# Expert values of an attention + mixture-of-experts kernel: from resident tiles to a DRAM scratch that is read back pair by pair

## The chip, the cores and the metric

The kernel runs on one core of a Trainium2 chip. The metric is the device time of one launch in microseconds (us). The kernel before took 1017.82 us, the median of three runs (1015.98 to 1018.09).

Names of the engines: PE is TensorE (matmuls; PEld its weight loads), DVE is VectorE, ACT is ScalarE, POOL is GpSimd, SP is SyncE, which in this kernel issues every DMA, in one queue and in program order.

## The reference

Eight sequences of 1024 tokens with 256 features pass one layer: attention in a linear form, a layer norm, a gated feed-forward block with 16 experts, a second layer norm.

```python
# attention: x is (8, 1024, 256)
qkv = x @ Wqkv + bqkv;  q, k, v = split(qkv)
q = q - q.mean(2);  k = k - k.mean(2)
q2 = q*q / (sum(q*q) + 1e-7);  q2 = q2 / norm(q2, over the features)
k2 = k*k / (sum(k*k) + 1e-7);  k2 = k2 / norm(k2, over the tokens)
kv = einsum('bnc,bnd->bcd', k2, v)
att = (v + einsum('bnc,bcd->bnd', q2, kv) / sqrt(N)) @ Wln + bln
x = layernorm(x + att)
# experts: E = 16, H = 128, D = 256
sel    = sigmoid(einsum('bsd,ed->bse', x, expert_sel))
scores = relu(einsum('bsd,edh->bseh', x, keys))
out    = einsum('bseh,ehv,bse->bsv', scores, values, sel)
x = layernorm(x + out)
```

All is float32. The last layer norm takes off the mean over the features, so the kernel takes the mean off the rows of `values` beforehand; "centered values" are these rows.

## The kernel before, in words

**Tiles and chunks.** The 8192 tokens are cut into 16 chunks of 512 (`CH`). Features lie on the partitions, tokens in the free dimension. Every float32 operand of a large product is split into a high and a low part (`h` and `l`), and a product is three matmuls: high by high, low by high, high by low.

**The expert part of a chunk.** For expert e, ffn1 (six matmuls of 512 columns, line 358) makes the hidden tile `h` from `keyh`, `keyl` and the normed tokens `ych`, `ycl`. `gated` (lines 1052 to 1057) then does three steps: DVE multiplies relu(h) by the gate, which lies broadcast over the partitions in `selb`; ACT copies the high part `sh`; DVE makes the low part `sl`. ffn2 (six matmuls, line 1137) multiplies `sh` and `sl` by the centered values `valh` and `vall` and adds into two PSUM tiles, `w0` and `w1`, over all 16 experts of the chunk. Experts go in pairs p = 0 to 7. From chunk 1 on, pairs 4 to 7 make their hidden tiles by a scheme with fewer products (`fast1`, lines 1075 to 1111, matmuls on line 1090), which needs sums of keys (`u_sums`, from a second load `ksr` of the keys) and of tokens (`u_t`).

**Everything else of a chunk** is spread among the expert pairs of an earlier chunk: the projections `kp` and `qp`, the products `ap` (tokens by squared keys) and `yp` (attention output), the transposes `qt`, the gates `sp`, and the column sums of the layer norms `yv` and `wv`.

**Who sets the order.** The functions only declare tasks (`add`) with an engine, a cost, a key (when it is wanted) and the buffers that they read and write. `Work.order` (lines 202 to 319) lays them out once, before anything is issued, and what it decides is the program order on every engine: an engine whose next instruction waits holds up all that is behind it. A buffer is given a tag, and each tag has a number of slots (`SB_SLOTS`, lines 41 to 44); a task that opens a buffer is placed only when a slot is free, and the real instruction waits on the last user of that slot.

**Values before the change.** `u_weights(g, key)` (lines 941 to 976) runs four times in chunk 0, for experts 4g to 4g+3. It loads keys (`kst`) and values (`vst`) through staging slots, splits the keys into `keyh` and `keyl`, takes the mean of each row of the values (`vst_m`), and writes `valh` (ACT, line 972) and `vall` (DVE, line 974). The tags `g0` to `g3` have four slots each of 4 KB per partition: two for keys and two for values. They stay for the whole kernel, so that ffn2 of all 16 chunks reads the same eight value tiles. `g2` and `g3` serve as staging for chunk 0 first (`kst`, `vst` of group 0; the tokens `xf`, `nf` of chunks 0 and 1).

**Other buffers that matter here.** `ld2` has three slots of 2 KB and holds, one after the other, `kst`, `vst`, `xf`, `nf` and `ksr`. `selb` has two slots: the gate rows of a pair are fetched from DRAM (`gates_of`, line 1030) when DVE has done the gates of the pair two before.

Of the kernel before, what the change touches and what calls it, by code (L numbers as in the profile page):

```python
# [23 lines left out]
LAG = 2.2  # L24
# [6 lines left out]
FAST_FROM = 1  # L31
FAST_AT = 0.39
AT_Y, AT_YEND, AT_X, AT_N, AT_K, AT_Q, AT_M, AT_END = 2.04, 4.17, 0.95, 0.19, 5.21, 12, 16.28, -0.91
AT_Q1, AT_K2, AT_W1, AT_W2, AT_W3, AT_SUMS, AT_SEL = -30, -19.9, -10.93, -7.7, 8.8, 8.58, 7
EAGER = 3.73
BOOST = 2.0
RESERVE = {"att": 1}
# [2 lines left out]

SB_SLOTS = {
    "ld2": 3, "xh": 2, "xl": 2, "s4": 4, "ych": 2, "ycl": 2, "sh": 2, "sl": 2, "selb": 2, "gt": 2, "t4": 6, "t2": 4,
    "v1": 2, "g0": 4, "g1": 4, "g2": 4, "g3": 4, "acc": 1, "asb": 1, "mh": 1, "ml": 1, "tiny": 14,
}
PS_SLOTS = {"h": 4, "att": 2, "w0": 1, "w1": 1}

# [1 line left out]
def f(ap):  # L48
    return ap.bitcast(F32)
# [273 lines left out]
def attn_ffn_kernel(ctx, tc, x, xT, wqT, wk, wvT, wlnT, bcols, brows, selT, keys, values, outT):  # L323
# [13 lines left out]
    def sbuf(tag, shape, name, dtype=F32):  # L337
        return work.buf(tag, shape, dtype, name)
# [75 lines left out]
        cbuf("bc", [P, 8]), cbuf("bkbc", [P, 1, D]), cbuf("bqbc", [P, 1, D]), cbuf("by", [P, 2]), cbuf("bvlbc", [P, D]),  # L414
    )
    eft, ewt, bls, blt = cbuf("eft", [P, 2, NE]), cbuf("ewt", [P, 2, P], FR), cbuf("bls", [P, 1]), cbuf("blt", [P, 1])
    keyh, keyl, valh, vall = {}, {}, {}, {}

    S.preload_act_table_set("natural_log_exp_and_others")

# [96 lines left out]
    def split(c, key, name, src, h, l, width):  # L517

        rows = h.shape[1]
        n = 1 if c < 2 else 2  # L520
        for i in range(n):
            s = slice(i * rows // n, (i + 1) * rows // n)
            part = None if n == 1 else i
            b = sbuf("g3" if c < 2 else "ld2", [P, rows // n, width], f"{name}{c}_{i}")
            add("D", 2.1 / n, key, lambda b=b, s=s: nc.sync.dma_start(out=b.ap, in_=src(s)), w=[b])
# [413 lines left out]


    def u_weights(g, key):
        for to, name in ((keyh, "keyh"), (keyl, "keyl"), (valh, "valh"), (vall, "vall")):
            to[g] = sbuf(f"g{g}", [P, 4, 2, P] if to in (keyh, keyl) else [P, 4, D], f"{name}{g}", FR)
        n = 1 if g == 0 else 2
        size = 4 // n
        for i in range(n):
            here = slice(i * size, (i + 1) * size)
            es = slice(4 * g + here.start, 4 * g + here.stop)
            tag = "g2" if g == 0 else "ld2"
            part = here if n > 1 else None  # L950
            kst = sbuf(tag, [P, size, 2, P], f"kst{g}_{i}")
            add("D", 2.1 / n, key, lambda kst=kst, es=es: nc.sync.dma_start(out=kst.ap, in_=keys[es].rearrange("e (k p) h -> p e k h", p=P)), w=[kst])
            add("S", c_act(size * D, plain=True), key + 1.2, lambda kst=kst, here=here: S.copy(keyh[g][:, here], kst.ap), r=[kst], w=[(keyh[g], part)])
            for j in range(2 // n):
                two = slice(here.start + 2 * j, here.start + 2 * j + 2)
                apply(key + 1.5, lambda two=two: keyl[g][:, two], lambda kst=kst, j=j: kst[:, 2 * j : 2 * j + 2], lambda two=two: f(keyh[g][:, two]),
                      ALU.subtract, CH, [kst, (keyh[g], part)], [(keyl[g], two)], "V" if g == 0 else spare(key))
        key += 1
        for i in range(n):
            here = slice(i * size, (i + 1) * size)  # L960
            es = slice(4 * g + here.start, 4 * g + here.stop)
            tag = "g2" if g == 0 else "ld2"
            vst = sbuf(tag, [P, size, D], f"vst{g}_{i}")
            add("D", 2.1 / n, key, lambda vst=vst, es=es: nc.sync.dma_start(out=vst.ap, in_=values[es].rearrange("e h v -> h e v")), w=[vst])
            m = tiny(f"vst{g}_{i}_m")
            for j in range(2 // n):
                two = slice(2 * j, 2 * j + 2)
                add("V", c_dve(CH), key + 1.2, lambda two=two, vst=vst, m=m: V.tensor_reduce(m[:, two], vst[:, two], AX.X, ALU.add), r=[vst], w=[(m, j)])
            add("V", 0.17, key + 1.3, lambda m=m: V.tensor_scalar(m[:, :size], m[:, :size], -1.0 / D, None, ALU.mult), r=[m], w=[m])
            for j in range(size):  # L970
                e = here.start + j
                add("S", c_act(D), key + 1.4, lambda j=j, e=e, vst=vst, m=m: S.activation(valh[g][:, e], vst[:, j], AF.Identity, bias=m[:, j : j + 1]),
                    r=[vst, m], w=[(valh[g], e)])
                add("V", c_dve(D, ptr=True), key + 1.8, lambda j=j, e=e, vst=vst, m=m: V.scalar_tensor_tensor(
                    vall[g][:, e], vst[:, j], m[:, j : j + 1], f(valh[g][:, e]), ALU.add, ALU.subtract),
                    r=[vst, m, (valh[g], e)], w=[(vall[g], e)], port=True)

# [55 lines left out]
    def u_pair(c, p):  # L1033
        key = NE * c + 2 * p
        if p == 0:
            wps[c] = [psum(f"w{v}_{c}", f"w{v}") for v in range(2)]
        gates_of(c, p, max(0, SOON - 2 * p) if c == 0 else 0)
        sel = selb[c, p]
        a, b = (sbuf(n, [P, 2, CH], f"{n}{c}_{p}", FR) for n in ("sh", "sl"))
        if c >= FAST_FROM and p in FAST_PAIRS:  # L1040
            fast1(c, p, key, sel, a, b)
        else:
            for i in range(2):
                plain1(c, 2 * p + i, key + i, sel, a, b)
# [67 lines left out]

    def ffn2_halves(c, e, key, a, b):

        g, i = e // 4, e % 2
        if e == NE - HALVED:
            rest[:] = [psum(f"rest{v}") for v in range(2)]

        def run(part):
            r = slice(part * CH // 2, (part + 1) * CH // 2)  # L1120
            for j, (w, x) in enumerate(((valh[g], a), (vall[g], a), (valh[g], b))):
                for v in range(2):
                    out = rest[v][:, : CH // 2] if part else wps[c][v][:, r]
                    T.matmul(out, w[:, e % 4, v * P : (v + 1) * P], x[:, i, r], start=part == 1 and e == NE - HALVED and j == 0,
                             stop=e == NE - 1 and j == 2)

        for part in range(2):
            add("T", c_mm(CH // 2, 6), key + LAG + part * HALVED, lambda part=part: run(part),
                r=[(valh[g], e % 4), (vall[g], e % 4), (a, i), (b, i)], w=rest if part else wps[c])

    def ffn2(c, e, key, a, b):
        g, i = e // 4, e % 2

        def run():
            for j, (w, r) in enumerate(((valh[g], a), (vall[g], a), (valh[g], b))):
                for v in range(2):
                    T.matmul(wps[c][v].ap, w[:, e % 4, v * P : (v + 1) * P], r[:, i], start=e == 0 and j == 0, stop=e == NE - 1 and j == 2)  # L1137

        t = add("T", c_mm(CH, 6), key + LAG, run, r=[(valh[g], e % 4), (vall[g], e % 4), (a, i), (b, i)], w=wps[c])
        if c == 0 and e < SOON:  # L1140
            work.goals[t] = -2.8 * e

# [263 lines left out]
```

## Time and profile before

| what | value |
|---|---|
| time, median of three runs | 1017.82 us (1015.98 to 1018.09) |
| profiled execution, span from first to last instruction | 1013.8 us |
| what lies around the span (median less span) | 4.0 us |
| PE busy | 1003.8 us |
| DVE, ACT, POOL busy | 792.9, 678.5, 488.5 us |
| DMA queue of SP | 98.48 MB, 30.4% of the 16 DMA engines' time |
| DMA issues of SP | 372 |
| granted TensorE clock, mean | 0.996 |

The page gives each engine's busy time, the DMA queues, the chain that ended last (followed back from the last instruction to what released each step) and the costliest groups of instructions. A matmul's end is modelled, so that a busy PE is not yet a PE at its pace; the distance from one matmul's start to the next shows the pace. The views used below are the table of stretches (busy time of each engine between two times, granted clock, share of the DMA engines), the timeline of one engine, the list of waits and the chain in order of time. All times in them count from the start of the span.

### The profile page before, as it was taken

Reading aid. Unit: us, or ns where it says so; the run is one execution under the profiler, and the core shown is the slowest. Engines: PE = TensorE matmul, PEld = TensorE weight load, DVE = VectorE, ACT = ScalarE, POOL = GpSimd, SP = SyncE. Lnnn points to the kernel's source line nnn. Section 1 sums busy time; section 2 is a strip of 40 time slices with the busy share of each in tenths; the row PEclk is TensorE's granted clock in tenths of the full one; section 3 lists DMA queues with packets and bytes.
Section 4 is the critical chain, followed back from the end, with each engine's and each line's share of the span. In section 5 each row is a group of like instructions: output and inputs, shape, how many; then the busy total and the mean of one; then the engine's idle time right before and its main releaser. Section 6 shows DMA issues by size and latency. Waiting matters only on the chain.

```text
span 1013.8 us, 16268 instructions
## 1 busy us (share of the span) xinstructions
PE 1003.8 (99%) x5709; PEld 868.9 (86%) x5709; DVE 792.9 (78%) x1363; ACT 678.5 (67%) x1515; POOL 488.5 (48%) x436
## 2 busy tenths in 40 slices
PE   9999999999999999999999999999999999999996
PEld 9978879888898988889888888988889888888886
DVE  7889888588776887768887688867888688686775
ACT  7767576676776767767676676757776675665543
POOL 1001685538564474655636475454754537333430
PEclk9999999999999999999999999999999999999998
DMA  6144433322241333323223232323323222223131
GB/s 203 56 124 125 120 98 118 94 97 93 83 126 65 116 94 104 99 89 97 94 91 110 86 105 70 116 96 102 105 75 104 94 85 75 93 85 105 64 125 42
DMA packets 65298, 99.52 MB, mean 98 GB/s; under 512 B 6336, under 2 KB 24896, under 8 KB 65216
## 3 DMA queue, kind: packets, MB, share of 16 engines
q1 hardware_dynamic: 65216, 98.48, 30.4%
q8 instruction: 45, 0.74, 0.3%
q14 instruction: 37, 0.30, 0.1%
HBM read 89.54 MB, written 8.91 MB: 97 GB/s over the span
## 4 chain that ended last, share of the span: by engine, by line
PE 92%; DVE 3%; POOL 2%; DMA 1%; ACT 1%; issue 1%; SPq 0%; POOLq 0%; DVEq 0%; ACTq 0%
PE w L1137 32%; PE h L358 17%; PE hx L1090 11%; PE yp L358 8%; PE qp L358 4%; PE hy L1090 4%; PE kp L358 4%; PE ap L358 4%; PE qt L771 1%; PE sp L358 1%; PE pm L358 1%; DMA ksr<-keys 1%; PE warm L435 0%; DVE sl L1057 0%; DMA xf<-xT 0%
## 5 line engine op out<-in xcount | busy, mean ns | idle before, releaser
L1137 PE MATMUL w<-sh,valh 128*128 128x512 f32 x504 | 157.9, 394 | 0.0
L1137 PE MATMUL w<-sh,vall 128*128 128x512 f32 x504 | 157.8, 394 | 0.0
L1137 PE MATMUL w<-sl,valh 128*128 128x512 f32 x504 | 157.6, 394 | 0.0
L1055 DVE SCALAR_TENSOR_TENSOR h<-h,selb 128x512 f32<-128x512 f32 x136 | 93.9, 692 | 29.6 <-PE h L358 24.9
L1137 PEld LDWEIGHTS w<-sl,valh 128*128 128x128 f32 x504 | 94.6, 188 | 22.4
L1137 PEld LDWEIGHTS w<-sh,vall 128*128 128x128 f32 x504 | 94.6, 188 | 22.0
L1056 ACT CAST sh<-h 128x512 fp32r<-128x512 f32 x136 | 74.2, 588 | 57.2 <-PE w L1137 46.2
L358 PE MATMUL h<-ych,keyh 128*128 128x512 f32 x272 | 110.4, 406 | 0.0
L358 PE MATMUL h<-ycl,keyh 128*128 128x512 f32 x272 | 108.3, 398 | 0.0
L358 PE MATMUL h<-ych,keyl 128*128 128x512 f32 x272 | 107.5, 395 | 0.0
L1057 DVE TENSOR_TENSOR sl<-h,sh 128x512 fp32r<-128x512 f32 x136 | 87.7, 682 | 22.4 <-ACT sh L1056 22.3
L1137 PEld LDWEIGHTS w<-sh,valh 128*128 128x128 f32 x504 | 86.0, 188 | 10.9
L389 POOL TENSOR_TENSOR k<-k,ks 128x512 f32<-128x512 f32 x25 | 30.9, 1256 | 102.4 <-DVE ks L566 102.4
L1109 DVE TENSOR_TENSOR hx<-hx,p 128x512 f32<-128x512 f32 x60 | 41.8, 696 | 29.9 <-ACT hy L1106 29.6
L389 POOL TENSOR_TENSOR ysq<-ysq 128x512 f32<-128x512 f32 x15 | 20.0, 1333 | 89.2 <-ACT ysq L891 89.2
L1151 POOL TENSOR_TENSOR w<-w,ycl 128x512 f32<-128x512 f32 x30 | 38.3, 1297 | 49.4 <-DVE w L1148 49.4
L358 PEld LDWEIGHTS h<-ych,keyl 128*128 128x128 f32 x272 | 51.5, 189 | 12.2
L358 PEld LDWEIGHTS h<-ycl,keyh 128*128 128x128 f32 x272 | 51.6, 190 | 10.7
L358 PEld LDWEIGHTS h<-ych,keyh 128*128 128x128 f32 x272 | 51.5, 189 | 10.9
L893 DVE SCALAR_TENSOR_TENSOR ycl<-yp,by,ych 128x512 fp32r<-128x512 f32 x32 | 24.0, 750 | 41.4 <-ACT ysq L891 41.4
L389 POOL TENSOR_TENSOR kss<-kss 128x512 f32<-128x512 f32 (+1 forms) x18 | 25.0, 1391 | 57.6 <-DVE gr L935 57.6
L1057 DVE TENSOR_TENSOR sl<-hx,sh 128x512 fp32r<-128x512 f32 x60 | 40.8, 681 | 15.1 <-ACT sh L1056 14.9
(511 smaller groups left out, 3204.6 us busy)
## 6 DMA issues: line engine op xcount, KB each, us to landing
selb<-sel SPq DMA_DIRECT2D x253, 256.0 KB, 3.4
xf<-xT SPq DMA_DIRECT2D x30, 256.0 KB, 2.8
outT<-w SPq DMA_DIRECT2D x15, 512.0 KB, 3.0
nf<-x SPq DMA_DIRECT2D x28, 256.0 KB, 4.7
kst<-keys SPq DMA_DIRECT2D x6, 256.0 KB, 3.3
vst<-values SPq DMA_DIRECT2D x6, 256.0 KB, 3.0
nf<-x SPq DMA_DIRECT2D x2, 512.0 KB, 7.6
ksr<-keys SPq DMA_DIRECT2D x4, 256.0 KB, 3.6
```

The costliest lines, as they stand in the source:

```text
L358: T.matmul(out, w, r, start=first and i == 0, stop=last and i == len(terms) - 1)
L389: fns = {e: (lambda e=e: ENG[e].tensor_tensor(out(), a(), b(), op)) for e in engines}
L771: T.transpose(o[:, t * P : (t + 1) * P], q[:, t, ct * P : (ct + 1) * P], ident.ap)
L893: add("V", c_dve(CH, ptr=True), k0 + 0.9, lambda t=t, jt=jt: V.scalar_tensor_tensor(yl[:, jt, :], t.ap, by[:, jt : jt + 1], f(yh[:, jt, :] ...
L1055: add("V", c_dve(CH), key + 0.1, lambda: V.scalar_tensor_tensor(at(t.ap), at(h.ap), 0.0, out(sel), ALU.max, ALU.mult), r=[h] + reads(sel), ...
L1056: add("S", c_act(CH, plain=True), key + 0.1, lambda: S.copy(out(a), at(t.ap)), r=[t], w=reads(a))
L1057: add("V", c_dve(CH), key + 0.1, lambda: V.tensor_tensor(out(b), at(t.ap), f(out(a)), ALU.subtract), r=[t] + reads(a), w=reads(b))
L1090: T.matmul(out(), wi, ri, start=first and i == 0, stop=True, skip_group_check=True)
L1109: add("V", c_dve(CH), key + 0.09, lambda: V.tensor_tensor(halves_(x.ap), halves_(x.ap), p5.ap.to_broadcast([P, 2, n]), ALU.add), r=[x, p5] ...
L1137: T.matmul(wps[c][v].ap, w[:, e % 4, v * P : (v + 1) * P], r[:, i], start=e == 0 and j == 0, stop=e == NE - 1 and j == 2)
L1151: add("G", c_pool(CH), key + 0.5, lambda v=v: G.tensor_tensor(w[:, v, :], w[:, v, :], f(ycl[c][:, v, :]), ALU.add), r=[(w, v), ycl[c]], w= ...
```

## The change

The centered values leave their resident tiles. `u_weights` writes both parts of an expert pair into one tile `vals` of 4 KB per partition (high and low by two experts by 256) under a new tag `vs` with four slots, and a DMA writes this tile into a DRAM buffer `vdram` (512 KB for each pair, eight pairs). Chunk 0 reads the tile that was just made. In every chunk from 1 on, `u_pair` opens a `vals` buffer for the pair and fetches it from `vdram` by one DMA of 512 KB, wanted six experts ahead (`AT_VALS`). The fetches stand in one line of dependences (`fetched`): the first comes after all the high parts were made, each other one after the fetch before it. The tags `g0` to `g3` go from four slots to two. The staging of `nf` for chunks 0 and 1 moves from `g3` to `vs`. The matmuls of ffn2 keep their number, shapes and order.

```diff
-AT_Q1, AT_K2, AT_W1, AT_W2, AT_W3, AT_SUMS, AT_SEL = -30, -19.9, -10.93, -7.7, 8.8, 8.58, 7
+AT_Q1, AT_K2, AT_W1, AT_W2, AT_W3, AT_SUMS, AT_SEL, AT_VALS = -30, -19.9, -10.93, -7.7, 8.8, 8.58, 7, 6
-    "v1": 2, "g0": 4, "g1": 4, "g2": 4, "g3": 4, "acc": 1, "asb": 1, "mh": 1, "ml": 1, "tiny": 14,
+    "v1": 2, "g0": 2, "g1": 2, "g2": 2, "g3": 2, "vs": 4, "acc": 1, "asb": 1, "mh": 1, "ml": 1, "tiny": 14,
...
-            b = sbuf("g3" if c < 2 else "ld2", [P, rows // n, width], f"{name}{c}_{i}")
+            b = sbuf(("g3" if name == "xf" else "vs") if c < 2 else "ld2", [P, rows // n, width], f"{name}{c}_{i}")
...
     def u_weights(g, key):
+        for to, name in ((keyh, "keyh"), (keyl, "keyl")):
+            to[g] = sbuf(f"g{g}", [P, 4, 2, P], f"{name}{g}", FR)
+        for p in (2 * g, 2 * g + 1):
+            vals[0, p] = sbuf("vs", [P, 2, 2, D], f"vals0_{p}", FR)
+            vdram[p] = work.buf("dram", [P, 2, 2, D], F32, f"vdram{p}")
...
+                fetched.append(add("S", c_act(D), key + 1.4, lambda j=j, to=to, o=o, vst=vst, m=m: S.activation(
+                    to[:, 0, o], vst[:, j], AF.Identity, bias=m[:, j : j + 1]), r=[vst, m], w=[(to, o)]))
+                add("V", c_dve(D, ptr=True), key + 1.8, lambda j=j, to=to, o=o, vst=vst, m=m: V.scalar_tensor_tensor(
+                    to[:, 1, o], vst[:, j], m[:, j : j + 1], f(to[:, 0, o]), ALU.add, ALU.subtract),
+                    r=[vst, m], w=[(to, o)], port=True)
+        for p in (2 * g, 2 * g + 1):
+            add("D", 2.1, key + 2.2, lambda p=p: nc.sync.dma_start(out=vdram[p].ap, in_=f(vals[0, p].ap)), r=[vals[0, p]], w=[vdram[p]])
...
     def u_pair(c, p):
+        if c:
+            vals[c, p] = sbuf("vs", [P, 2, 2, D], f"vals{c}_{p}", FR)
+            fetched[:] = [add("D", 2.1, key - AT_VALS, lambda: nc.sync.dma_start(out=f(vals[c, p].ap), in_=vdram[p].ap),
+                              r=[vdram[p]], w=[vals[c, p]], after=fetched)]
...
     def ffn2(c, e, key, a, b):
-            for j, (w, r) in enumerate(((valh[g], a), (vall[g], a), (valh[g], b))):
+            for j, (w, r) in enumerate(((0, a), (1, a), (0, b))):
                 for v in range(2):
-                    T.matmul(wps[c][v].ap, w[:, e % 4, v * P : (v + 1) * P], r[:, i], start=e == 0 and j == 0, stop=e == NE - 1 and j == 2)
+                    T.matmul(wps[c][v].ap, u[:, w, i, v * P : (v + 1) * P], r[:, i], start=e == 0 and j == 0, stop=e == NE - 1 and j == 2)
```

More of the change, by code (lines that the diff above doesn't have):

```diff
@@ L416, in attn_ffn_kernel @@
     eft, ewt, bls, blt = cbuf("eft", [P, 2, NE]), cbuf("ewt", [P, 2, P], FR), cbuf("bls", [P, 1]), cbuf("blt", [P, 1])
-    keyh, keyl, valh, vall = {}, {}, {}, {}
+    keyh, keyl, vals, vdram, fetched = {}, {}, {}, {}, []
     S.preload_act_table_set("natural_log_exp_and_others")
@@ L941, in u_weights @@
     def u_weights(g, key):
-        for to, name in ((keyh, "keyh"), (keyl, "keyl"), (valh, "valh"), (vall, "vall")):
-            to[g] = sbuf(f"g{g}", [P, 4, 2, P] if to in (keyh, keyl) else [P, 4, D], f"{name}{g}", FR)
+        for to, name in ((keyh, "keyh"), (keyl, "keyl")):
[3 more added lines that the diff above has]
+            vdram[p] = work.buf("dram", [P, 2, 2, D], F32, f"vdram{p}")
         n = 1 if g == 0 else 2
@@ L970, in u_weights @@
             for j in range(size):
[L971 to L976, printed above, removed]
+                e = 4 * g + here.start + j
+                to, o = vals[0, e // 2], e % 2
+                fetched.append(add("S", c_act(D), key + 1.4, lambda j=j, to=to, o=o, vst=vst, m=m: S.activation(
[5 more added lines that the diff above has]
+            add("D", 2.1, key + 2.2, lambda p=p: nc.sync.dma_start(out=vdram[p].ap, in_=f(vals[0, p].ap)), r=[vals[0, p]], w=[vdram[p]])
     sums_h, sums_l, th, tl = {}, {}, {}, {}
@@ L1113, in ffn2_halves @@
     def ffn2_halves(c, e, key, a, b):
-        g, i = e // 4, e % 2
+        u, i = vals[c, e // 2], e % 2
         if e == NE - HALVED:
@@ L1120, in run @@
             r = slice(part * CH // 2, (part + 1) * CH // 2)
-            for j, (w, x) in enumerate(((valh[g], a), (vall[g], a), (valh[g], b))):
+            for j, (w, x) in enumerate(((0, a), (1, a), (0, b))):
                 for v in range(2):
                     out = rest[v][:, : CH // 2] if part else wps[c][v][:, r]
-                    T.matmul(out, w[:, e % 4, v * P : (v + 1) * P], x[:, i, r], start=part == 1 and e == NE - HALVED and j == 0,
+                    T.matmul(out, u[:, w, i, v * P : (v + 1) * P], x[:, i, r], start=part == 1 and e == NE - HALVED and j == 0,
                              stop=e == NE - 1 and j == 2)
@@ L1128, in ffn2_halves @@
             add("T", c_mm(CH // 2, 6), key + LAG + part * HALVED, lambda part=part: run(part),
-                r=[(valh[g], e % 4), (vall[g], e % 4), (a, i), (b, i)], w=rest if part else wps[c])
+                r=[(u, i), (a, i), (b, i)], w=rest if part else wps[c])
     def ffn2(c, e, key, a, b):
-        g, i = e // 4, e % 2
+        u, i = vals[c, e // 2], e % 2
         def run():
-            for j, (w, r) in enumerate(((valh[g], a), (vall[g], a), (valh[g], b))):
+            for j, (w, r) in enumerate(((0, a), (1, a), (0, b))):
                 for v in range(2):
-                    T.matmul(wps[c][v].ap, w[:, e % 4, v * P : (v + 1) * P], r[:, i], start=e == 0 and j == 0, stop=e == NE - 1 and j == 2)
-        t = add("T", c_mm(CH, 6), key + LAG, run, r=[(valh[g], e % 4), (vall[g], e % 4), (a, i), (b, i)], w=wps[c])
+                    T.matmul(wps[c][v].ap, u[:, w, i, v * P : (v + 1) * P], r[:, i], start=e == 0 and j == 0, stop=e == NE - 1 and j == 2)
+        t = add("T", c_mm(CH, 6), key + LAG, run, r=[(u, i), (a, i), (b, i)], w=wps[c])
         if c == 0 and e < SOON:
```

## The prediction, made before the changed kernel ran

> **What bounds the kernel now.** I read the page first, then the list of waits, then the starts of PE's matmuls one by one, then the table of stretches and the DMA views.
>
> ```profile
> span 1013.8 us, 16268 instructions
> ...
> PE 1003.8 (99%) x5709; PEld 868.9 (86%) x5709; DVE 792.9 (78%) x1363; ACT 678.5 (67%) x1515; POOL 488.5 (48%) x436
> ...
> q1 hardware_dynamic: 65216, 98.48, 30.4%
> ...
> PE 92%; DVE 3%; POOL 2%; DMA 1%; ACT 1%; issue 1%; SPq 0%; POOLq 0%; DVEq 0%; ACTq 0%
> ```
>
> The chain that ended last is PE for 92%. A busy PE need not be at its pace, so the starts decide (timeline of PE, one row per matmul; then the same view at the only place after 64 us where PE waited):
>
> ```profile
> 71.31 0.39 PE L358 MATMUL yp<-xh,wyh 128*128 128x512 f32 x1
> 71.54 0.40 PE L358 MATMUL yp<-xl,wyh 128*128 128x512 f32 x1
> 71.77 0.40 PE L358 MATMUL yp<-xh,wyl 128*128 128x512 f32 x1
> ...
> 148.50 0.40 PE L358 MATMUL sp<-ycl,ewt 128*128 128x512 f32 x1
> 149.78 0.39 PE L1090 MATMUL hx<-th,ksh 128*128 128x256 f32 x1 [0.88 <-ACT p L1100]
> ```
>
> A matmul of 512 columns starts 0.23 us after the one before, one of 256 columns 0.115 us. I went along all starts from 63 us to the last chunk's end: the one gap over 0.1 us is the 1.28 us from 148.50 to 149.78, some 1.05 us more than a matmul takes. So between 63 and 1003 us PE has work at full pace, with nothing to win but that 1.05 us. A change that keeps PE's work can only add waits, or take away that one.
>
> The table of stretches (PE, PEld, DVE, ACT, POOL busy, granted clock, share of the DMA engines, GB/s):
>
> ```profile
> 48.00:64.00 16.00, 16.00 (x77) 11.81 (x77) 13.16 (x36) 13.18 (x36) 0.00 (x0) 0.89 0.32 99
> 64.00:80.00 16.00, 16.00 (x81) 13.27 (x80) 14.15 (x29) 9.44 (x20) 0.00 (x0) 1.00 0.50 148
> 96.00:112.00 16.00, 16.00 (x85) 13.62 (x84) 16.00 (x28) 7.22 (x14) 6.94 (x5) 1.00 0.41 117
> 400.00:640.00 240.00, 240.00 (x1369) 207.90 (x1369) 187.65 (x308) 166.42 (x370) 136.92 (x116) 1.00 0.30 98
> ```
>
> Two things are to be seen. From 96 to 112 us, in chunk 0, DVE has not one idle moment: there the first chunk is close to being set by DVE. And at 64 to 80 us, with the DMA engines at 0.50, PE keeps its 0.23 us (the three rows above lie there).
>
> **The change part by part.**
>
> *PE's work.* The built program has the same matmuls in the same order, but for three places: in chunk 0 `kp_0` and `kp_1` for chunk 3 move behind ffn2 of expert 5; in chunk 1 six `hx` matmuls move ahead of a `kp`; in the last chunk expert 6's ffn1 moves ahead of two ffn2. From chunk 2 to 14 every engine but SP has the order of before, bar a few DVE swaps at the ends. PE gets 120 more waits, one for each fetch. In the steady stretch 216 matmuls of 512 columns carry a wait that is met and 1716 carry none: both start a median 0.232 us after their predecessor. Cost 0.
>
> *The fetches, 15 chunks of 8.* The question is how early SP may issue each. A slot is free when ffn2 of the pair four before is done; SP is then free if nothing older on its queue waits. I put the fetches into SP's order and read the times from chunks 5 and 6 (timeline of SP; pieces of the chain):
>
> ```profile
> 411.06 0.32 SPq L938 DMA_DIRECT2D sel<-gr  x1
> ...
> 459.72 1.82 SPq L525 DMA_DIRECT2D nf<-x  x2
> ```
> ```profile
> 409.53 1.39 PE w L1137 x6
> ...
> 436.68 1.40 PE w L1137 x6
> ...
> 453.36 1.40 PE w L1137 x6
> ...
> 460.89 1.37 PE w L1137 x6
> ...
> 476.35 1.39 PE w L1137 x6
> ```
>
> Pair 0 of chunk 6: its slot is that of pair 4, whose ffn2 ends at 409.53 + 1.39 = 410.92; the fetch stands behind the gate store `sel` (411.06 + 0.32), so it goes out at 411.4 and is used at 436.68: 25 us of lead. The shortest is pair 5: slot free at 453.36 + 1.40 = 454.76, used at 476.35, 21.6 us. What a fetch takes is not in the trace; the nearest rows are these (KB, median us to landing):
>
> ```profile
> selb<-sel SPq DMA_DIRECT2D x253, 256.0 KB, 3.4
> ...
> outT<-w SPq DMA_DIRECT2D x15, 512.0 KB, 3.0
> ...
> vst<-values SPq DMA_DIRECT2D x1, 512.0 KB, 7.0
> nf<-x SPq DMA_DIRECT2D x2, 512.0 KB, 7.6
> ```
>
> 3.0 us is a store of the same size in the steady part, 7.6 us a load in the crowded first 16 us. I take 4, and even 7.6 is a third of the lead. Exposed: 0; it would take more than 21 us.
>
> The Trainium skill, in "TensorE: Matmul & The Clock Gate", section "HAM oscillation — how this bites in real kernels", says that a DMA wait of over some 3.4 us between matmuls makes PE start again at half clock. This trace has half clock in the row of 48 to 64 us (0.89): eight matmuls at 0.427 us. By that rule one such exposure in each of 15 chunks would cost some 15 x 8 x 0.195 = 23 us beside the waits; by the leads above it is nothing.
>
> *Queued behind a fetch.* SP waits in order. Pair 6's fetch waits until 460.89 + 1.37 = 462.3; behind it stand the two `nf` loads, issued at 459.7 before, now 2.6 us later. ACT first reads them at 479.8 and they land in 5.0 us: covered. `selb` stands ahead of its pair's fetch or 2 us behind an older one; its lead to DVE's gates is 9 us at least (issued 421.2, used 430.3) against 3.4 us to land. Covered up to a landing of 9 us.
>
> *The DMA engines.* 120 fetches and 8 stores of 512 KB are 67.1 MB on 98.48 MB; at the same rate per byte the share goes from 30.4% to 51%. The 64 to 80 us row shows that load with PE at pace. Cost 0; upper end as in rival 2.
>
> *Start.* DVE, ACT and PE keep their order to about 58 us. The stores of pairs 0 and 1 wait for low parts that end at 35.1 and 39.0 us, ahead of the next load (held until 41.4 us by a slot). Cost 0.
>
> *Chunk 0, 84 to 107 us.* Pairs 4 to 7 must wait for a `vs` slot, so their centering moves later and holds staging slots longer; `xf` and `kst` come some 5 to 15 us later. (a) `xf` now waits for `nl` to end (86.0 and 86.6), lands 2.8 us later, and DVE's two `xl` end by about 91.7; PE wants them at 92.1. Cost 0, upper 0.8. (b) `kp_1` now ends at 95.0 and DVE must add the bias, scale and split until the second `k2l` is done, which the second `ap` group wants at 106.74. Between stand 13 DVE instructions of 0.60 us and about 0.8 us of small ones, 8.6 us, starting at 96.4 to 98.1 (POOL's two `keyl` share DVE's port; `gr` in before took 1.17 instead of 0.6 beside POOL, 1.1 us for two). End: 105.0 to 107.8. Cost 0 to 1.1, I take 0.2, as the middle lies at PE's time.
>
> *Chunk 0 to 1, 110 to 150 us.* (c) The stores of pairs 6 and 7 wait for DVE at 112.0 and 112.9; behind them the first `ksr` goes out at 113.3 instead of 110.8, after 1.8 MB of others; landing 3.0 to 7.6 us gives 116 to 121 against 115.2. POOL's and ACT's work from it (`tu`, `th`, `ksl`) ends near 126 at worst; ACT's `sh` behind it is wanted at 132.4, `hx` at 147. Cost 0, upper 1.0. (d) The wait at 148.5: POOL stood 1.06 us on a late `ksr` (142.05 to 143.11), which made `ysq`, then two ACT copies late, and behind those the copies that `hx` needs. In the new POOL order the two `xl` and `ysq` stand ahead of that `ksr`: `ysq` ends at 146.7 instead of 147.8, ACT's copies at 148.0, the `hx` copies at 148.75, when PE arrives (148.73). Gain 0.9, between 0 and 1.05.
>
> *Tail.* Expert 6's ffn1 at 968.3 needs the slot of expert 2, free at 967; the work is the same. Cost 0.
>
> Sum against the profiled execution: 1013.8 + 0.2 - 0.9 = 1013.1 us, best end 1012.8, worst 1013.8 + 0.8 + 1.1 + 1.0 = 1016.7. The median of the runs is 4.0 us above the span: 1017.1 us, with 1016.8 and 1020.7 as ends of the known terms.
>
> **The rivals.**
>
> *1. Slower: DVE falls behind in chunk 0.* Place: the second `k2l` before `ap`, wanted at 106.74. For it: DVE is at 16.00 of 16 there, has no slack, and its end was 105.0 to 107.8. Against it: DVE has four instructions fewer in all. Price: every us that DVE (or the `xf` landing ahead of it) is late past 106.7 is a us of PE. If four instructions there take 1.17 instead of 0.6 us beside POOL, and the four late low parts of 0.45 us fall ahead of it, that is 4 x 0.57 + 4 x 0.45 = 4.1 us. It decides from 2.9 us of lateness on (+2.0 after the gain of 0.9): 1019.8 to 1021.0.
>
> *2. Slower: the steady chunks pay.* A gate row that lands later than 9 us after its issue stops DVE, then PE. For it: the DMA share goes to 51%. Against it: 0.50 was seen with landings of a few us. Price: 0.5 us for each of 15 chunks is 7.5 us, less the gain of 0.9: 1024.4.
>
> *3. Faster by more than 2 us.* The only gap after 63 us is 1.05 us, and the first 63 us keep their order; only the spread of the runs (2.1 us in three) can show more. 1015.
>
> **How the numbers follow.** 0.2% of 1017.8 is 2.0 us, about what a measurement of this kernel can tell from no change. Chances: the forecast, within it, 0.62; rival 1, 0.19; rival 2, 0.09; rival 3, 0.10. So faster 0.10, same 0.62, slower 0.28. The likeliest time is 1017.1; its own range 1015.8 to 1019.8. The range reaches into rival 3 to 1015.2 and over rival 1 to the start of rival 2, 1023.0.
>
> **What would show it.** Right: matmuls of line 1147 still 0.23 us apart; from 200 us on the same 121.4 us for two chunks (`yp` at 318.07 and 439.48); PE waiting for no DMA of `vals`; the 0.88 us idle at `hx` gone; DMA share near 50%, fetches landing in 3 to 5 us. Wrong: PE idle before `ap` or `kp` between 90 and 110 us behind DVE; `hx` waiting for POOL or ACT past 148 us; SP waiting on PE with a late `selb` behind it.

## The result: slower by 0.32%, and the profile after

The changed kernel took 1020.25 us, the median of eight runs (1019.52 to 1021.90), against 1017.71 us for the kernel before in the same comparison (1015.45 to 1018.50). The ratio taken from all runs is 1.0032, with a 95% interval of 1.0022 to 1.0042; the two medians alone give 1.0025. Its profiled execution has a span of 1017.6 us (1013.8 before). The spans lie further apart than the medians because single executions of one kernel differ by up to 3 us, and the profiled one of the kernel before was among the quicker. The forecast was 1017.1 us and "no change"; the first rival was 1019.8 to 1021.0 us.

The page of the changed kernel, the lines that answer to those shown of before:

```profile
span 1017.6 us, 16514 instructions
...
PE 1006.2 (99%) x5709; PEld 869.9 (85%) x5709; DVE 794.6 (78%) x1359; ACT 679.4 (67%) x1515; POOL 493.1 (48%) x440
...
q1 hardware_dynamic: 83648, 165.60, 49.1%
...
PE 91%; DVE 5%; ACT 2%; POOL 1%; issue 1%; DVEq 0%; POOLq 0%; ACTq 0%
```

The queue moves 165.60 MB instead of 98.48 and takes 49.1% of the DMA engines (the forecast was 51%). Neither SP's queue nor a DMA is in the chain any more, and DVE's share went from 3% to 5%. What PE waited for between 64 and 1004 us (list of waits: total, times, longest):

```profile
PE ap L358 <- DVE k2l L389: 0.9, 1, 0.9
PE hy L1100 <- ACT hy L1116: 0.6, 1, 0.6
PE qt L771 <- DVE mt L700: 0.5, 1, 0.5
PE hy L1100 <- ACT hy L1109: 0.2, 1, 0.2
```

No fetch is among them. Where the time went is best read by landmarks: the first matmul of `yp` of every chunk, in the changed kernel less the same in the kernel before. It is +0.01 us at 71 us, +1.78 at 137, +3.09 at 197, +3.20 at 260, +3.30 at 439, +3.47 at 745 and +3.63 at 922. So 3.1 of the 3.6 us arise between 71 and 197 us, in the first chunk and on the way into the second; the twelve chunks from there to 922 us add 0.5 us in all. The table of stretches (PE, PEld, DVE, ACT, POOL busy, granted clock, DMA share, GB/s) shows the same:

```profile
96.00:112.00 16.00, 15.12 (x78) 12.64 (x77) 15.97 (x28) 9.38 (x20) 7.74 (x7) 1.00 0.32 105
112.00:128.00 16.00, 16.00 (x87) 13.65 (x86) 13.52 (x23) 10.55 (x28) 11.25 (x14) 1.00 0.75 252
400.00:640.00 240.00, 240.00 (x1365) 207.91 (x1365) 187.16 (x309) 166.06 (x370) 135.31 (x116) 1.00 0.50 164
```

From 96 to 112 us DVE is full, as before, but PE now stands 0.88 us; from 400 to 640 us, at a DMA share of 0.50, PE has no idle time.

Going along the starts of all matmuls from 63 to 200 us, and taking off what each one needs at full pace, the idle time of PE is this (us; the last column is an experiment told below):

| place in the changed kernel | waits for | changed | same order, no transfers |
|---|---|---|---|
| `ap`, 106.6 | DVE `k2l` | 1.03 | 0.93 |
| `qt`, 134.7 | DVE `mt` | 0.69 | 0.63 |
| `hy`, 154.8 | ACT `hy` | 0.71 | 0.69 |
| `kp`, `hx`, `hy`, `hx`, 158 to 173 | ACT `hy` at one of them | 1.02 | 1.02 |

The sum is 3.45 us, where the kernel before had 1.05 us at `hx` (148.5): 2.4 us more. Idle times below 0.15 us each make up the rest of the 3.1 us, some 0.7 us.

### The profile page after: what moved, and what is told of

Its sections match the earlier page's. It is cut to its first block, busy times and chain, and to the rows that moved or that the text cites. A ratio compares the mean times of both kernels' runs of the same rounds, so it can differ in the third digit from the quotient of the medians.

```text
span 1017.6 us, 16514 instructions
## 1 busy us (share of the span) xinstructions
PE 1006.2 (99%) x5709; PEld 869.9 (85%) x5709; DVE 794.6 (78%) x1359; ACT 679.4 (67%) x1515; POOL 493.1 (48%) x440
## 3 DMA queue, kind: packets, MB, share of 16 engines
q1 hardware_dynamic: 83648, 165.60, 49.1%
## 4 chain that ended last, share of the span: by engine, by line
PE 91%; DVE 5%; ACT 2%; POOL 1%; issue 1%; DVEq 0%; POOLq 0%; ACTq 0%
PE w L1147 32%; PE h L358 17%; PE hx L1100 10%; PE yp L358 8%; PE qp L358 4%; PE ap L358 4%; PE hy L1100 4%; PE kp L358 4%; PE qt L771 1%; PE sp L358 1%; PE warm L435 1%; PE pm L358 1%; DVE sl L1067 1%; DVE h L1065 1%; DVE vals L978 1%
## 5 line engine op out<-in xcount | busy, mean ns | idle before, releaser
L1147 PE MATMUL w<-sh,vals 128*128 128x512 f32 x1008 | 275.2, 395 | 0.0
L1147 PEld LDWEIGHTS w<-sh,vals 128*128 128x128 f32 x1008 | 180.6, 188 | 33.0 <-DVE w L1158 0.2
L1147 PE MATMUL w<-sl,vals 128*128 128x512 f32 x504 | 158.0, 394 | 0.0
L1147 PEld LDWEIGHTS w<-sl,vals 128*128 128x128 f32 x504 | 94.6, 188 | 22.8
L358 PE MATMUL h<-ycl,keyh 128*128 128x512 f32 x272 | 107.8, 396 | 0.0
L358 PE MATMUL h<-ych,keyl 128*128 128x512 f32 x272 | 107.8, 396 | 0.0
L558 ACT ACTIVATE k<-k,c_zero 128x256 f32<-128x256 f32 x56 | 28.2, 507 | 28.8 <-DVE k L585 28.8
L1116 ACT COPY hy<-hx 128x256 f32<-128x256 f32 x60 | 21.5, 358 | 38.5 <-PE hx L1100 37.3
L389 POOL TENSOR_TENSOR q<-q,qy 128x512 f32<-128x512 f32 x27 | 27.6, 1042 | 34.9 <-ACT sh L1066 30.2
```

Of the source, the lines that this page charges most:

```text
L358: T.matmul(out, w, r, start=first and i == 0, stop=last and i == len(terms) - 1)
L389: fns = {e: (lambda e=e: ENG[e].tensor_tensor(out(), a(), b(), op)) for e in engines}
L558: S.activation(q[:, t, :], q[:, t, :] if src is None else src[:, t % 2 * D : (t % 2 + 1) * D], AF.Square, bias=c_zero.ap, accum_out=s[:, t ...
L1116: add("S", c_act(n, plain=True), key + 0.07, lambda: S.copy(y1(), x1()), r=[x], w=[y])
L1147: T.matmul(wps[c][v].ap, u[:, w, i, v * P : (v + 1) * P], r[:, i], start=e == 0 and j == 0, stop=e == NE - 1 and j == 2)
```

## The experiments

Two theories stood against each other. **A:** the transfers cost nothing; the loss is the order that the planner lays for chunk 0, once it has to reckon with four `vs` slots and with DMAs that it charges 2.1 us each. **B:** the transfers cost it, by their traffic and by the waits of SP on the stores. All runs below were timed against the kernel before on the same chip (1016.55 to 1017.38 us); with the changed kernel they are compared by these ratios. The first 71 us vary by up to 2.5 us between executions, and the granted clock with them (0.89 from 48 to 64 us in the changed kernel, 0.79 in run 5), so that in the profiles idle times are compared and not absolute times.

### 1. The order of the changed kernel without its transfers

The planner sees the same tasks and lays the same order on every engine. When they are issued, stores and fetches are left out and the values stay in eight resident tiles `kept`.

```diff
-            add("D", 2.1, key + 2.2, lambda p=p: nc.sync.dma_start(out=vdram[p].ap, in_=f(vals[0, p].ap)), ...
+            add("D", 2.1, key + 2.2, lambda p=p: None, ...
-            fetched[:] = [add("D", 2.1, key - AT_VALS, lambda: nc.sync.dma_start(out=f(vals[c, p].ap), in_=vdram[p].ap), ...
+            fetched[:] = [add("D", 2.1, key - AT_VALS, lambda: None, ...
-                    T.matmul(wps[c][v].ap, u[:, w, i, ...
+                    T.matmul(wps[c][v].ap, keep(e // 2)[:, w, i, ...
```

> The order of every engine is that of the changed kernel, but no store and no fetch is issued and the eight value tiles stay resident (32 KB a partition), so there is no traffic, no wait of SP on a store and no wait for a slot of vs. Theory A: 2 to 3 us slower than before, ratio 1.002 to 1.003, with the gap at ap near 106.6 us. Theory B: the time of the kernel before to 0.1%, and no gap there.

Measured: 1019.06 us (1018.07 to 1020.80), ratio 1.0024 (1.0014 to 1.0033). Its list of waits of PE, from 64 us on (line numbers are 9 higher, 3 higher in the helpers):

```profile
PE ap L361 <- DVE k2l L392: 0.8, 1, 0.8
PE hy L1109 <- ACT hy L1125: 0.5, 1, 0.5
PE qt L780 <- DVE mt L709: 0.5, 1, 0.5
PE hy L1109 <- ACT hy L1118: 0.2, 1, 0.2
```

The same four waits, in the same order and to 0.1 us as long; the table above sets the idle times side by side. In this execution the start took 2.0 us longer; from there to 160 us POOL's instructions follow those of the changed kernel at a distance of 1.95 to 1.99 us (`ksu` at 152.38 against 150.43 us, `ksl` at 156.95 against 154.97). For this order, then, neither the traffic nor SP's waits on the stores matter in chunk 0: A holds, B falls. In particular the late `ksr` is not the stores' doing. Its first load went out at 116.23 us in the changed kernel, behind two stores that waited for DVE, and here, with no store at all, at 117.84: a mere 0.3 us sooner once the 1.95 us are taken off.

Behind 197 us the two runs part. There the landmarks of this run gain on the kernel before: +4.92 us at 197, with the late start in it, and +3.95 at 922, while the changed kernel loses 0.5 us over the same stretch. The changed kernel's ratio (1.0032 against 1.0024 here) leaves room for some 0.8 us that is not the order's; the two intervals overlap.

### 2. The transfers in the order of the kernel before

The other half of the cross: all stores and fetches are issued, and ffn2 reads what they bring, but the plan charges almost nothing for them and `vs` has a fifth slot. PE, DVE, ACT and POOL then keep the order of the kernel before, instruction for instruction.

```diff
-AT_VALS = 6
+AT_VALS = 4
-"vs": 4
+"vs": 5
-            add("D", 2.1, key + 2.2, lambda p=p: nc.sync.dma_start(out=vdram[p].ap, ...
+            add("D", 0.01, key + 8, lambda p=p: nc.sync.dma_start(out=vdram[p].ap, ...
-            fetched[:] = [add("D", 2.1, key - AT_VALS, ...
+            fetched[:] = [add("D", 0.01, key - AT_VALS, ...
```

> All eight stores and all 120 fetches stay and are read by ffn2; the plan charges each of them 0.01 us instead of 2.1, wants the stores 5.8 experts later and the fetches four experts ahead, and vs has five slots. With that the order of PE, DVE, ACT and POOL is the one of the kernel before, instruction for instruction. Theory A (the loss is the order of the first chunk, in which DVE reaches its work late; the transfers are covered): the time of the kernel before to 0.1%, 1017.0 to 1018.5 us, with the gap of 1.05 us ahead of hx near 148 us back and none at ap near 106.6 us. Theory B (the loss is the transfers themselves: SP's waits on the stores and 512 KB per pair): slower than before by 2 to 3 us, as the changed kernel is, with gaps between 106 and 172 us.

Measured: 1024.41 us (1022.62 to 1026.82), ratio 1.0073 (1.0058 to 1.0088). Both theories missed: A said no loss, B a third of it. Its waits of PE from 64 us on:

```profile
PE hx L1100 <- ACT p L1110: 4.0, 1, 4.0
PE w L1147 <- ACT sh L1066: 1.2, 1, 1.2
PE h L358 <- DVE sl L1067: 0.9, 1, 0.9
PE qt L771 <- DVE mt L700: 0.5, 1, 0.5
```

Two pieces of its chain in order of time (start, duration, what):

```profile
112.07 7.49 DMA ksr<-keys
...
143.39 5.84 DMA ksr<-keys
```

In the order of before the loads `ksr` stand on the chain that leads to `hx`. The same pieces of the kernel before:

```profile
110.82 4.35 DMA ksr<-keys
...
138.91 4.07 DMA ksr<-keys
```

In run 2 the first went out 1.25 us later, 1.0 us behind a store and 0.5 us behind a fetch of 512 KB each, and took 3.1 us longer; the last went out 4.5 us later, when some 4 us had been lost already, and took 1.8 us longer. POOL makes `ksu` from them; the chain goes on from the first over `tu`, `sh` and `sl` to `h`, from the last over `xl`, `ysq` and ACT's copies to `hx`. So a third theory, **C**: the transfers are harmless only where the order leaves `ksr` off the chain; in the order of before they are not.

### 3. Four slots instead of five

```diff
-"vs": 5
+"vs": 4
```

> As the run with all transfers in the order of before, but vs has four slots as in the changed kernel, which moves 30 of 1220 DVE tasks between 67 and 119 us of the plan and three PE tasks; from chunk 1 on the order is that of before. If the fourth against the fifth slot makes the order that costs (a part of theory A): slower than before by 1 to 3 us, with gaps between 106 and 172 us. If the charge of 2.1 us in the plan makes it: the time of before to 0.1%. Theory B: 2 to 3 us slower.

Measured: 1022.11 us (1020.30 to 1024.89), ratio 1.0050 (1.0035 to 1.0065).

```profile
PE hx L1100 <- ACT p L1110: 2.6, 1, 2.6
PE qp L358 <- DVE q L733: 1.6, 1, 1.6
PE ap L358 <- DVE k2l L389: 0.5, 1, 0.5
```

`ap` and `qp` waiting for DVE are new against run 2 and come with the fourth slot taken away, as expected of the order in A; the wait at `hx` is that of run 2, and it makes the whole larger than any of the expectations. The run does not separate the two cleanly, because with four slots the order moves too.

### 4. Less work for DVE ahead of `k2l`

The one place of A that can be tested by itself is `ap`. Nothing is moved; three DVE instructions become short.

```diff
-        newton(key + 0.4, lambda: v[:NE], a, lambda: rs[:NE], 1.0, ...
+        few = slice(0, 64 if c == 1 else CH)
+        newton(key + 0.4, lambda: v[:NE, few], lambda: a()[:, few], lambda: rs[:NE, few], 1.0, ...
```

> The changed kernel with one thing less: the three DVE instructions of the Newton step for chunk 1's gates (at 92.9, 94.7 and 96.6 us, 0.60, 1.28 and 1.67 us apart) work on 64 of 512 columns; for the other columns the refinement of the reciprocal root is left out. Order and transfers are unchanged. Theory A (DVE is what PE waits for at ap): k2l ends 2.5 to 3 us sooner than 107.7 us, the gap of 1.03 us at 106.6 us goes, and the time falls by 0.8 to 1.7 us against the changed kernel, ratio to before 1.0015 to 1.0024. Theory B: nothing moves by more than 0.3 us, ratio 1.003.

Measured: 1018.70 us (1018.04 to 1020.64), ratio 1.0021 (1.0011 to 1.0030), by the ratios some 1.1 us less than the changed kernel, though the two intervals overlap. `k2l` ended at 106.81 us, in an execution whose start took 0.6 us longer: 1.5 us sooner than in the changed kernel, not the 2.5 to 3 expected.

```profile
PE hy L1101 <- ACT hy L1117: 0.5, 1, 0.5
PE hy L1101 <- ACT hy L1110: 0.2, 1, 0.2
PE qt L771 <- DVE mt L700: 0.2, 1, 0.2
```

The wait at `ap` is gone and the one at `qt` fell from 0.5 to 0.2 us; those at `hy` stayed. So the first two are DVE's lateness. At `hy` both came 1.5 us sooner, counted from the first `yp` after 71 us, PE and the copy that it waits for, so that the wait (0.69 us of idle time against 0.71) is not made by the lateness at `ap`.

### 5. `k2l` ahead of other DVE work

```diff
-            apply(key + 4 + g * 0.3, lambda tt=tt: l[:, tt, :], ...
+            apply(key + 4 + g * 0.3 - (1.5 if c == 3 else 0), lambda tt=tt: l[:, tt, :], ...
```

> The changed kernel with one key changed: the second k2l of chunk 3, for which PE waits at ap (1.03 us at 106.6 us), is wanted earlier and stands three DVE instructions further ahead (ahead of two steps of gr and one sl). As a consequence the planner also hands two squares of POOL (L389 k<-k, 105.4 and 107.3 us) to DVE behind it and in chunk 1 PE takes kp before hx of pair 5. Theory A: k2l ends 1.8 to 3.4 us sooner than 107.7 us, the gap at ap is gone; what follows after 112 us is open, since the order there changes too. Time against the changed kernel -0.5 to -1.5 us, ratio 1.0017 to 1.0027. Theory B (DVE's order is not it): the gap stays at 1 us.

Measured: 1020.78 us (1018.69 to 1023.21), ratio 1.0037 (1.0024 to 1.0051). One wait is left in the whole list:

```profile
PE qp L358 <- DVE q L733: 3.0, 1, 3.0
```

`ap` does not wait any more, as A expected; the time did not follow. What was put behind, two squares taken over from POOL and the low parts of the values, now stands ahead of `q`, and `qp` waits 3.0 us for that. In this run DVE is busy for 16.97 of the 17 us from 98 to 115 us; what one instruction gained there, another lost, and the wait moved from `ap` to `qp`.

### 6. A fetch that costs nothing in the plan

```diff
-            fetched[:] = [add("D", 2.1, key - AT_VALS, ...
+            fetched[:] = [add("D", 0.01, key - AT_VALS, ...
```

> The changed kernel with one number of the plan changed: a fetch is charged 0.01 us instead of 2.1. Up to 127 us every engine keeps the order of the changed kernel; then the load ksr of pair 6 stands one place earlier in SP's queue, and in chunk 1 PE takes kp before hx of pair 5 again, as before the change. Theory A in two parts (first DVE late at ap, then hx and hy of chunk 1 taken ahead of their operands): the gaps of 1.0 us near 106.6 and 0.7 us near 134.7 stay, the gaps between 154 and 173 us (1.7 us together) shrink below 0.8, and the time falls by 0.7 to 1.5 us against the changed kernel, ratio to before 1.0017 to 1.0026. If the second part is not PE's order but POOL and ACT being late by themselves: the gap comes back at another place near 150 us with 1 us or more, and the ratio stays at 1.003.

Measured: 1021.95 us (1020.46 to 1022.21), ratio 1.0042 (1.0028 to 1.0055).

```profile
PE wv L358 <- DVE ycl L893: 2.1, 1, 2.1
PE ap L358 <- DVE k2l L389: 1.1, 1, 1.1
PE qt L771 <- DVE mt L700: 0.5, 1, 0.5
PE yp L358 <- DVE q2l L775: 0.2, 1, 0.2
```

The losses at `ap` and `qt` stayed, as they should. Those at `hy` are gone, but a wait of 2.1 us at `wv` took their place: the second expectation, not the first. PE's order at that place is therefore not the cause by itself; what made `ycl` late here was not followed up.

### 7. Own slots for `ksr`

Theory C says what to do in the order of before: load `ksr` before the fetches begin. It shares three slots (`ld2`) with other loads; the change freed 16 KB a partition, of which these four slots and the fifth of `vs` take 12.

```diff
-        b, u = sbuf("ld2", [P, 2, 2, P], f"ksr{p}"), ...
-        add("D", 1.05, key, lambda: nc.sync.dma_start(out=b.ap, in_=keys[2 * p : 2 * p + 2]...
+        b, u = sbuf("kr", [P, 2, 2, P], f"ksr{p}"), ...
+        add("D", 1.05, key - 2, lambda: nc.sync.dma_start(out=b.ap, in_=keys[2 * p : 2 * p + 2]...
```

With the edits of run 2 (five slots of `vs`, 4 of `kr`):

> As the run with all transfers in the order of before (five slots of vs), but the four ksr loads have four slots of their own (2 KB each, from the room that the change freed) and are wanted two experts earlier, so that they are issued at about 85 to 107 us of the plan, ahead of the fetches. PE keeps its order, 3 DVE and 14 POOL tasks move near 119 to 149 us. Theory C (in the order of before the 8 us were lost because ksr, on the chain to hx, landed in 7.5 and 5.8 us behind stores and fetches, where it took 4.35 and 4.07): the gap of 4.1 us at hx near 152.5 us goes, those between 123 and 137 us too, and the time is that of before within 0.15%, 1015.5 to 1018 us; below it if the gap of 1.05 us at hx that before has goes as well. If the loss was in waits of SP on stores and slots for other loads: still 2 us or more slower than before.

Measured: 1017.01 us (1015.10 to 1017.80), ratio 0.9998 (0.9989 to 1.0007). PE's only wait of over 0.2 us from 64 us on:

```profile
PE qp L358 <- DVE q L733: 0.7, 1, 0.7
```

The whole loss of run 2 is back, by an edit to four loads of 256 KB, with the same 120 fetches and 8 stores. The loads took no less time here (4.3 to 6.9 us to land), but went out at 89.5 to 116.5 us in place of 112.1 to 143.4, and so were done before the chain needed them. That is what C says. The edit also takes the four loads out of the slots that `xf` and `nf` use, and moves 3 DVE and 14 POOL tasks; the run does not separate these.

The same slots in the order of the changed kernel (`"vs": 4, "kr": 4`, `key - 4`):

> The changed kernel with four slots of its own for ksr, wanted four experts earlier; PE's order is unchanged, DVE's is unchanged up to 118 us. Theory A says that the gap at ap near 106.6 us (1.03 us) is DVE's and stays, and that the POOL work on ksr is done earlier, so that the gap at 154.8 us (0.7 us) and those up to 173 us shrink: 0.5 to 1.5 us faster than the changed kernel, ratio 1.0017 to 1.0027. If ksr is what makes all of it: the time of before, 1.000.

Measured: 1018.93 us (1018.20 to 1020.61), ratio 1.0021 (1.0012 to 1.0030), as expected in time, though the interval overlaps that of the changed kernel.

```profile
PE hx L1100 <- ACT p L1110: 0.7, 1, 0.7
PE qt L771 <- DVE mt L700: 0.5, 1, 0.5
PE w L1147 <- ACT sh L1066: 0.4, 1, 0.4
```

But not in place: the idle time at `ap`, which I expected to stay, fell from 1.03 to 0.18 us, although DVE's order up to there is the same. The reason is told in the last section; it is POOL's `keyl`, which starts at another moment.

### 8. `ksr` earlier still

`key - 4` and `key - 8` in place of `key - 2`, in the order of before.

> As the run with the order of before and own slots for ksr, with ksr wanted four experts earlier instead of two (the plan issues the loads at 83 to 99 us). About 20 DVE and 16 POOL tasks move between 88 and 149 us. Theory C: no gap at hx near 150 us; 1015.5 to 1018 us. The gap of 0.9 us at qp near 115 us, where PE waited for DVE, may go or grow: it depends on which DVE work the planner put ahead of q.

Measured: 1019.29 us (1017.12 to 1020.18), ratio 1.0018 (1.0009 to 1.0026). No wait at `hx`, but 3.1 us at `qp` for DVE's `q`: the planner moved 20 DVE tasks, and it is run 5 again. The time lies above the 1015.5 to 1018 us that C expected: with `ksr` out of the way, the order on DVE decides.

> The same with ksr wanted eight experts earlier (the plan issues the loads at 15 and 82 to 85 us), so that none stands near a store or a fetch. Theory C: no gap at hx near 150 us, 1015.5 to 1018 us.

Measured: 1016.65 us (1014.26 to 1018.13), ratio 0.9993 (0.9985 to 1.0002). Its waits of PE from 64 us on:

```profile
PE wv L358 <- POOL keyl L389: 0.2, 1, 0.2
```

One row of its table of stretches:

```profile
96.00:112.00 16.00, 16.00 (x84) 13.55 (x83) 16.00 (x31) 8.95 (x19) 10.94 (x9) 1.00 0.48 144
```

DVE is full from 96 to 112 us here too, but PE stands nowhere in the row: a full engine does not by itself mean a wait. All transfers of the change are in it, and PE waits less than in the kernel before. It is 0.4% faster than the changed kernel (0.9993 / 1.0032); against the kernel before the interval holds 1, so that it cannot be told from it. The 1.05 us at `hx` that before had is all that the waits after 64 us left to win.

## Why the prediction was wrong

**What held.** The fetches: they landed in a median of 4.4 us (forecast 4), no matmul waited for one, and the two-chunk distance of `yp` is 121.49 us (321.12 to 442.61) against 121.40. The share of the DMA engines is 49.1%. The start, the tail (0.1 us) and step (a), `xf` to `kp`, cost nothing. Step (c) is right for the end, if not for its place: `ksr` went out at 116.23 us and not at 113.3, and no load of `ksr` is on the chain of the changed kernel from 84 to 180 us. The rule on the half clock, weighed at 0 for the fetches, was rightly left at 0: no wait of the changed kernel after 64 us is longer than 0.9 us.

**Step (b), mis-sized: 0.2 us taken, 1.03 measured.** The interval given for the end of the second `k2l`, 105.0 to 107.8 us, held; it ended at 107.71. In the kernel before it ended at 102.30 us (a piece of its chain):

```profile
101.63 0.67 DVE k2l L389
```

I took the middle, because the range lay about PE's time, and so made a price of almost nothing out of a range that reached 1 us past the point of need, on an engine that was busy 16.00 us of 16. The count itself was right: 13 instructions of 0.60 us and some 0.6 us of small ones. But the bias add from which they count started at 98.24 us, just past the late end of the range for it, because `rs` and `gr` ahead of it had been held up beside POOL by 0.68 and 1.07 us; and `k2l` itself was held up by 1.0 us. The working had 1.1 us for two such hold-ups; these three are 2.8 us. Against the kernel before, two `gr` and two `sl` stand ahead of that `k2l` that did not, 4 x 0.6 = 2.4 us. Together that is 5.2 of the 5.4 us by which `k2l` ended later; smaller moves, for and against, are left out.

**A step that is missing: `qt`, 0.69 us.** DVE's lateness was followed to `ap` and no further. The chain of the changed kernel goes on from `k2l` over the four late low parts of the values to `mt`, for which `qt` waits:

```profile
112.52 3.29 DVE vals L978 x3
...
134.76 0.40 DVE mt L700
```

The low parts run from 109.6 to 115.8 us in DVE's queue, 0.4 us each alone and 0.95 to 1.6 us here, where POOL is busy too. Rival 1 named these low parts, but ahead of `k2l`; the sum of the forecast did not have them.

**Step (d), wrong: a gain of 0.9 us forecast, a loss of 0.7 measured.** The wait at 148.5 us did go away, but not as forecast. POOL's `ysq` was to end at 146.7 us by the new order; it ended at 147.76, where the kernel before had 147.79, and ACT's copies `yv2s` behind it start at the same time in both (first lines below). PE came to that place 1.8 us later, after its waits at `ap` and `qt`: the lateness covered the wait, and nothing was gained. And what is late next was not asked. The timeline of ACT in the changed kernel:

```profile
147.79 1.25 ACT L787 COPY yv2s<-ysq 64x512 f32<-64x512 f32 x2 [0.50 <-POOL ysq L389]
...
153.57 0.51 ACT L1004 CAST ksh<-ksu 128x384 fp32r<-128x384 f32 x1 [1.36 <-POOL ksu L389]
153.99 0.29 ACT L1005 CAST keyh<-ksu 128x128 fp32r<-128x128 f32 x1
154.19 1.06 ACT L1066 CAST sh<-h 128x512 fp32r<-128x512 f32 x2
155.15 0.38 ACT L1116 COPY hy<-hx 128x256 f32<-128x256 f32 x1
```

The same view of the kernel before:

```profile
147.83 1.25 ACT L787 COPY yv2s<-ysq 64x512 f32<-64x512 f32 x2 [2.31 <-POOL ysq L389]
...
152.91 0.36 ACT L1106 COPY hy<-hx 128x256 f32<-128x256 f32 x1
154.34 0.51 ACT L998 CAST ksh<-ksu 128x384 fp32r<-128x384 f32 x1 [1.08 <-POOL ksu L389]
```

Before, the copy `hy` stood ahead of `ksh`. Now `ksh` stands ahead of it, waits 1.36 us for POOL's `ksu`, and two `sh` follow; PE gets `hy` at 155.5 and stands 0.71 us, then four times more for 1.02 us. So 1.73 us in place of 1.05. That ACT's order is this cause was read from the trace and is not shown by a run of its own; run 4 shows only that it is not DVE's lateness at `ap`, and run 7 that with `ksu` done earlier the waits after 150 us fall to 0.86 us.

**The sum.** In place of +0.2 - 0.9 the profiles show +1.03 at `ap`, +0.69 at `qt` and +0.68 in chunk 1 (1.73 for 1.05), with 0.7 us of small idle times, 0.5 us in the later chunks and 0.1 in the tail: 3.7 of the 3.8 us between the two spans. The known terms of the forecast reached to 1020.7 us; the range given with it ended at 1019.8, below them, and 1020.25 lies between.

**The rivals.** Rival 1 had the place, DVE in chunk 0, and its time, 1019.8 to 1021.0 us, holds the measured one. Its sum did not happen: it asked for 2.9 us or more of lateness at `ap` less a gain of 0.9, and there were 1.03 us at `ap`, no gain, and losses at `qt` and `hy` that it did not have. So its place was right and its time in part luck. Rival 2 did not happen: 0.5 us over twelve chunks, and not 0.5 us for each. That rest is no wait. It goes with the four slots of `vs`: from 197 to 922 us the six kernels with transfers and four slots lose 0.3 to 0.6 us against the kernel before, the four with five slots and the same transfers gain 0.04 to 0.2. The mean distance of two neighbouring matmuls of 512 columns in that stretch is 0.2334 us in the changed kernel, 0.2331 in the kernel before and with five slots, and 0.2327 in run 1, which has no transfers and other tiles for the values. Why stays open.

**What neither had:** that the transfers do cost, up to 8 us, where `ksr` lies on the chain (run 2). The order that the planner laid for four slots and for DMAs of 2.1 us kept the changed kernel from it, and cost 3 us. What in the plan does which was not separated: with the fetches alone at 0.01 us (run 6) no wait at `hx` came, with fetches and stores at 0.01 us and four slots (run 3) it did.

## What to carry to other kernels

A change that only adds hidden transfers can cost through the order that a planner lays around them: separate the two by issuing the new order without the transfers and the old order with them. Where a range ends past the point of need on an engine that is busy in every microsecond, let the forecast's range reach as far as its late end, and ask at each wait that goes away which instruction is late next in that queue. Before adding traffic to a queue, look for the loads that already stand on the chain, and give those their own buffers first.

## What the runs showed of the hardware

**DVE held up by POOL.** One DVE instruction, the same in shape, order and neighbours, in two runs. First the changed kernel, the timeline of DVE:

```profile
96.57 1.74 DVE L374 SCALAR_TENSOR_TENSOR gr<-rs,gr 16x512 f32<-16x512 f32 x1
...
106.03 1.68 DVE L389 TENSOR_TENSOR k2l<-k,k2h 128x512 fp32r<-128x512 f32 x1
```

and of POOL:

```profile
96.48 1.29 POOL L389 TENSOR_TENSOR keyl<-kst,keyh 128x512 fp32r<-128x512 f32 x1 [0.98 <-ACT keyh L956]
105.40 2.91 POOL L389 TENSOR_TENSOR k<-k 128x512 f32<-128x512 f32 x2 [7.63 <-ACT kss L597]
```

Then the changed kernel with own slots for `ksr`, where POOL's `keyl` starts later; DVE:

```profile
97.07 0.67 DVE L374 SCALAR_TENSOR_TENSOR gr<-rs,gr 16x512 f32<-16x512 f32 x1
```

and POOL:

```profile
100.67 2.42 POOL L389 TENSOR_TENSOR keyl<-kst,keyh 128x512 fp32r<-128x512 f32 x1 [4.67 <-ACT keyh L956]
```

`gr` takes 0.67 us alone and 1.74 us when it starts 0.09 us after a `keyl` of 1.29 us: it ends 0.54 us after POOL is done (98.31 against 97.77). The wait of 1.07 us is about what was left of POOL's instruction (1.20 us), though DVE's own works on 16 partitions only. The Trainium skill, "SBUF — State Buffer", section "Who interferes with whom", says this: a DVE instruction with two inputs in SBUF and a GpSimd instruction that reads SBUF exclude each other, and the one that issues second waits until the first is done. The rows agree. That a start moved by some microseconds decides this accounts for the 0.18 us at `ap` in run 7: `gr` took 1.07 us less, the second `k2l` 0.39 us less, the first 0.51 and `rs` 0.09 us more, and 0.86 us in all is what `ap` waited less.

**The clock after a wait.** Run 2 has the longest wait of PE, 3.96 us. Its table of stretches around that wait (columns as above):

```profile
152.00:156.00 4.00, 0.92 (x4) 0.39 (x3) 3.94 (x4) 1.07 (x2) 2.89 (x2) 1.00 0.45 127
156.00:158.00 2.00, 1.13 (x5) 1.13 (x6) 0.55 (x1) 1.41 (x5) 1.26 (x1) 0.69 0.56 216
158.00:160.00 2.00, 2.00 (x7) 1.64 (x7) 0.13 (x1) 0.86 (x2) 1.06 (x1) 0.50 0.18 62
```

PE starts again at 156.87 us at half clock and keeps it until about 160: four matmuls of 512 columns 0.43 us apart instead of 0.232. After the waits of 3.0 us (run 5) and 3.1 us (`key - 4` in run 8) every matmul has its full pace. So here a wait a microsecond longer cost some 1.4 us beside the wait (4 x 0.2 and six of 256 columns at 0.21 instead of 0.115). The Trainium skill puts the limit at about 3.4 us ("TensorE: Matmul & The Clock Gate", section "HAM oscillation — how this bites in real kernels"), which lies between the two. A long wait is not the only way to the half clock: the kernel before shows it in its row of 48 to 64 us (0.89), and its longest wait of PE is 1.1 us.
